# Four chained image layers on one core: when the first image and the constants are loaded, and where PE is given filling matmuls

## The chip, the cores and the metric

The kernel runs on one core of a Trainium2 chip. The metric is the device time of one execution in microseconds (us); smaller is better. The engines are named as the profile names them: PE is TensorE (its weight loads are PEld), DVE is VectorE, ACT is ScalarE, POOL is GpSimd, and SP is SyncE, whose queue issues every DMA of this kernel.

## What is computed

The input `x` holds 32 images of 56 x 56 pixels with 96 channels, float32. Four layers follow each other, and each image goes through them by itself:

```
layer 0   rw = sigmoid(mean over pixels(x) @ Wr + br)            # 4 expert weights for each image
          h  = relu(bn1(x @ (sum of rw[e] * Wpw[e]) + bias))      # 96 -> 384 channels
          h  = relu(bn2(3x3 depthwise(h, sum of rw[e]*Wdw[e])))   # 384 channels
          x  = x + bn3(h @ (sum of rw[e] * Wpwl[e]) + bias)       # 384 -> 96
layer 1   x  = x + 5x5 depthwise(x, a fixed kernel)
layer 2   x  = bn(1x1(3x3 depthwise(relu(x))))
layer 3   shifted-window attention (7x7 windows, 3 heads) and an MLP 96 -> 384 -> 96, both residual
```

## The kernel before

**Stages.** For each image `b` the kernel has four stages: `stage_router` (load the image, mean, expert weights, mixed weights), `stage_conditional` (the rest of layer 0), `stage_depthwise` (layers 1 and 2), and `stage_swin` (layer 3). At step `s` the router of image `s`, the conditional stage of image `s-1`, the depthwise stage of `s-2` and the swin stage of `s-3` are mixed with each other (lines 1469 to 1483). In layer 0, ACT and DVE do the 3x3 depthwise convolution: tap 0 is an ACT copy with a scale, and the other eight are DVE `scalar_tensor_tensor` instructions on 128 x 784 values, called taps below. PE does the 1x1 convolutions, the depthwise convolutions of layers 1 and 2 (as small banded matrices), the transposes, the attention and the MLP.

**The order is planned.** The stages don't issue instructions. They record them in a `Recorder` (line 261). `Recorder.order()` (line 339) then plays the whole program through once with a table of costs (`COST`, line 146) and gives each engine its instructions in the order in which its queue would start them; `give()` (line 482) issues them in that order. On the chip each engine works strictly in that order, and semaphores hold an instruction until its inputs are there and its buffer is free. So what is fixed in advance is the order on each engine, and the times come from the chip.

**Filling matmuls.** Where the plan finds PE without work for over 250 ns (`SPARE_AFTER`, line 161), `order()` puts in a matmul of the 128 x 128 identity with itself into a free PSUM bank (lines 447 to 458). Nobody reads it. It is called a filler below. Each is two MATMUL records in the profile. It waits on the chip, as any matmul does, until the bank that the plan gave it has been read by its last reader. All 8 PSUM banks are one ring.

**The beginning.** `tile_conv_seq_kernel` (line 491) first loads the constants of all four layers and works on them (lines 545 to 714): on SP some 55 loads one after the other, on POOL a dozen memsets and the powers of `rsqrt` (line 558), on DVE the batch-norm factors, the corrections of `band5` (line 640), and those of `pw` and `wo` (lines 652 to 685). The recorded work comes behind all of that on every queue, so the load of the first image (line 732) is issued after the last constant. Scratch space for the constants lies in `h2`, a buffer of layer 0 (line 537).

**The router.** `stage_router` loads an image in one DMA of 1176 KB, and ACT sums it in two passes of 1568 columns each (lines 734 to 737); DVE makes `pooled` and `pooled_w`, PE multiplies with `wr`, and the mixed weights `wmix` follow. The plan puts ACT's passes of images 0 and 1 in the order image 0, image 1, image 0, image 1.

Of the kernel before, what the change touches and what calls it, by code (L numbers as in the profile page):

```python
# [158 lines left out]

TO_TENSOR = {"vector": 1500, "gpsimd": 1500, "scalar": 1000, "sync": 700}  # L160
SPARE_AFTER = 250
SHARING = 1.36


# [96 lines left out]
class Recorder:  # L261
# [77 lines left out]
    def order(self):  # L339
# [66 lines left out]
        def begin(w):  # L406
            nonlocal count
            for b in w.needs:
                if b.slot is None:
                    b.ring.free.sort()  # L410
                    b.slot = b.ring.free.pop(0)[1]
                    b.ring.begun += 1
            result.append(w)
            w.start = now
            e = w.engine
            if e == "gpsimd" or w.calls[0][0] == "scalar_tensor_tensor":
                running[e] = {"work": w, "left": w.ns, "since": now, "rate": 1.0}
                share(now)
                return
            free[e] = now + w.ns  # L420
            heapq.heappush(events, (free[e], count, None))
            heapq.heappush(events, (free[e] + w.landing, count + 1, w))
            count += 2
            if e == "tensor":
                heapq.heappush(events, (free[e] + SPARE_AFTER, count, None))
                count += 1

        left = len(self.work)
        spares = 0
        while left:  # L430
            for e in self.ENGINES:
                if free[e] > now:
                    continue
                held = []
                while queues[e]:
                    item = heapq.heappop(queues[e])
                    w = self.work[item[1]]
                    if not available(w):
                        held.append(item)
                        continue  # L440
                    begin(w)
                    left -= 1
                    if e == "tensor":
                        spares = 0
                    break
                else:
                    if e == "tensor" and self.spare and now >= free[e] + SPARE_AFTER and self.spare[2].free:
                        lhs, rhs, ring = self.spare
                        w = Work(e, 0.0)
                        b = Buffer(ring)  # L450
                        operands = View(b, ring.tiles[0])[:, : rhs.shape[1]], lhs, rhs
                        w.calls.append(("matmul", operands, {"start": True, "stop": True}))
                        w.ns = cost(e, "matmul", operands, {})
                        w.needs, w.starts, w.uses, w.writes = [b], [b], [b], [b]
                        b.users[w], b.left, b.owner = True, 1, w
                        spares += 1
                        assert spares < 10000, "no work can start"
                        begin(w)
                for item in held:
                    heapq.heappush(queues[e], item)  # L460
            assert events, "no work can start"
            now = events[0][0]
            ready = []
            while events and events[0][0] <= now:
                _, _, w = heapq.heappop(events)
                if isinstance(w, tuple):
                    put(w[0])
                elif isinstance(w, dict):

                    if w["end"] == now and running.get(w["work"].engine) is w:  # L470
                        del running[w["work"].engine]
                        w["work"].end = now
                        done(w["work"], now)
                        share(now)
                elif w is not None:
                    done(w, now)
            for v in ready:
                heapq.heappush(events, (v.ready, count, (v,)))
                count += 1
        return result  # L480

    def give(self, tc):
        with tc.manual_schedule():
            for w in self.order():
                for method, args, kw in w.calls:
                    args = [v.found() if isinstance(v, View) else v for v in args]
                    kw = {k: v.found() if isinstance(v, View) else v for k, v in kw.items()}
                    getattr(getattr(self.nc, w.engine), method)(*args, **kw)  # L488
# [3 lines left out]
def kernel(  # L492
# [37 lines left out]
    if general:  # L530
# [2 lines left out]
        tops = ring("top", [PK, NP], 4)  # L533
        dens = ring("den", [PK, NP], 4)


    room = h2s.tiles[0].rearrange("p k n -> p (k n)")
    taken = [0]

    def scratch(rows, n):  # L540
        taken[0] += n
        return room[:rows, taken[0] - n : taken[0]]


    ident = const.tile([P, P], F32, name="ident")
# [2 lines left out]
    nc.gpsimd.memset(ones, 1.0)  # L548
    mhalf = const.tile([P, 4], F32, name="mhalf")
    nc.gpsimd.memset(mhalf, -0.5)  # L550
    mhalves = scratch(P, C)
    nc.gpsimd.memset(mhalves, -0.5)

    def rsqrt(dst, src, eps, scale=1.0):
# [75 lines left out]
    nc.vector.tensor_copy(experts[:, :, 9, :], c384[:, :, V_BPW : V_BPW + E])  # L630
    nc.vector.tensor_copy(experts[:, :, 10, :], c384[:, :, V_BDW : V_BDW + E])


    band5 = load([P, NG, 10, 32], layouts["k5"], "band5")
    centre = scratch(P, 64).rearrange("p (n c) -> p n c", n=2)
    nc.sync.dma_start(out=centre, in_=layouts["centre"])
    for g in range(NG):
        for n in range(2):
            at = 5 * n + 2
            nc.vector.tensor_tensor(band5[:, g, at], band5[:, g, at], centre[:, n], ALU.add)  # L640
    band3 = load([P, NG, 6, 32], layouts["k3"], "band3")


    pw = const.tile([C + 1, CM], F32, name="pw")
    nc.sync.dma_start(out=pw[:C, :C], in_=a["L2_conv_pw_kernel"].rearrange("a b c f -> (a b c) f"))

    def wide(name, keep=False):
        t = const.tile([P, C], F32, name=name) if keep else scratch(P, C)
        nc.sync.dma_start(out=t, in_=a[name].partition_broadcast(P))
        return t  # L650

    inv2 = wide("L2_conv_moving_var")
    rsqrt(inv2, inv2, BN_EPS)
    nc.vector.tensor_tensor(inv2, inv2, wide("L2_conv_gamma"), ALU.mult)
    dwb = scratch(C, P)
    nc.vector.tensor_scalar(dwb, ones[:C].to_broadcast([C, P]), col(U_DWB), None, ALU.mult)
    pt = mm.tiles[4]
    nc.tensor.matmul(pt[:, :C], dwb, pw[:C, :C], start=True, stop=True)
    bias2 = scratch(P, C)
    nc.vector.tensor_tensor(bias2, pt[:, :C], wide("L2_conv_pw_bias"), ALU.add)  # L660
    nc.vector.tensor_tensor(bias2, bias2, wide("L2_conv_moving_mean"), ALU.subtract)
    nc.vector.tensor_tensor(bias2, bias2, inv2, ALU.mult)
    nc.vector.tensor_tensor(bias2, bias2, wide("L2_conv_beta"), ALU.add)
    nc.vector.tensor_tensor(pw[:C, :C], pw[:C, :C], inv2[:C], ALU.mult)
    nc.vector.tensor_copy(pw[C:, :C], bias2[C : C + 1])

    def centre_outputs(w):

# [2 lines left out]
        nc.vector.tensor_scalar(mean, mean, 1.0 / C, None, ALU.mult)  # L671
        nc.vector.tensor_scalar(w[:, :C], w[:, :C], mean, None, ALU.subtract)

    centre_outputs(pw)


    wq = load([C, C], a["L3_conv_wq"], "wq")
    wk = load([C, C], a["L3_conv_wk"], "wk")
    wv = load([C, C], a["L3_conv_wv"], "wv")
    wo = const.tile([C + 1, CM], F32, name="wo")  # L680
    nc.sync.dma_start(out=wo[:C, :C], in_=a["L3_conv_wo"])
    nc.sync.dma_start(out=wo[C:, :C], in_=a["L3_conv_bo"].rearrange("(o c) -> o c", o=1))
    centre_outputs(wo)
    if not general:
        nc.vector.tensor_scalar(wo[:C], wo[:C], -1.0, None, ALU.mult)
    w1 = load([C, M], a["L3_conv_w1"], "w1")
    w2 = load([P, NB, C], a["L3_conv_w2"].rearrange("(k p) f -> p k f", p=P), "w2")
    b2 = wide("L3_conv_b2", True)
    if general:
        masks = load([PK, 2, NP * PK], layouts["mask"].rearrange("l q j k -> q l (j k)"), "masks")  # L690
    else:
        keep_last = load([P, NP, WT], layouts["keep_last"], "keep_last")
        keep_column = load([P, WT], layouts["keep_column"], "keep_column")

        slots = ring("slots", [C, NWIN, SLOT], 3)

        exps = ring("exps", [P, NH, NP, PK], 2)
        for t in slots.tiles + kTs.tiles + exps.tiles:
            nc.gpsimd.memset(t, 0.0)
        ones32 = const.tile([P, HD], F32, name="ones32")  # L700
        nc.gpsimd.memset(ones32, 1.0)

    for t in x1s.tiles + x2s.tiles + [h1.tiles[0] for h1 in h1s]:
        nc.gpsimd.memset(t, 0.0)
    for t in filtereds.tiles + oTs.tiles:
        nc.gpsimd.memset(t[C:], 1.0)

    for t in lnsqs.tiles:
        nc.gpsimd.memset(t[:, :, C:], C * LN_EPS)
    for u in (U_LN1G, U_LN2G):
        nc.vector.tensor_scalar(col(u), col(u), math.sqrt(C), None, ALU.mult)

# [12 lines left out]
    def stage_router(b):  # L728

        xT = chip.new(xTs).part(*range(NROW))  # L730
        sums = new_small("sums", [C, 2])
        chip.sync.dma_start(out=xT, in_=x[b])
        yield 3
        for q in range(2):
            part = xT[:, q * HALF * W : (q + 1) * HALF * W].part(*range(4 * q, 4 * q + 4))
# [733 lines left out]
    for step in range(B + 3):  # L1469
# [11 lines left out]
        if step < B:  # L1481
            stages.append((stage_router(step), 12, when("router", step)))
        interleave(stages)
    chip.give(tc)


def build(nc, shapes, batch):
# [41 lines left out]
```

## Time and profile before

| what | value |
|---|---|
| time, median of 3 runs | 5219.56 us (5214.70 to 5220.35) |
| the profiled execution: time, span | 5218.23 us, 5216.4 us |
| mean clock granted to PE | 0.987 |
| ACT busy | 3841.3 us, 74% |
| POOL busy | 3041.9 us, 58% |
| fillers, MATMUL records, whole span | 1746, in which PE was busy for 249.3 us |
| of these from 0 to 60 us | 100 records, 15.4 us |
| from 60 to 470 us | 684 records, 92.7 us |
| from 470 to 4930 us | 620 records, 95.7 us |
| from 4930 us to the end | 342 records, 45.5 us |

The span is the time from the first to the last instruction of the program on the chip; the execution's own time is 1.8 us longer. A view named "chain of waits" starts at the last instruction and goes back at each step to what released it, or to the instruction before it on its engine. In the timeline a row is a group of equal instructions: start, length, engine, line, operation, `out<-in`, shapes, count, and in brackets how long the engine was idle before and what ended that. Line 488 is the line of `give()` that issues all planned work, so planned instructions are told apart by their tiles: `banks<-ident` is a filler, and `banks<-ident,lnd` is a real transpose. Matmuls are pipelined and their ends are modelled, so PE's busy time is longer than the time between starts.

### The profile page before, as it was taken

The page shows a single profiled execution, that of the slowest core. Times are in us where ns is not written, and L with a number is a line of the kernel's source. Part 1 is how long each engine was busy: PE and PEld are TensorE (multiplying, and loading weights), DVE is VectorE, ACT ScalarE, POOL GpSimd, SP SyncE. Part 2 cuts the span into 40 slices and gives each one's busy share as a digit, 9 for nine tenths or more (in the row PEclk, how much of TensorE's full clock was granted, in tenths as well). Part 3 has the DMA queues.
Part 4 walks back from the last instruction along what each step waited for, and adds up shares of the span by engine and source line. Part 5 has one row for each costly group of instructions (what it writes and reads, how often), then busy time and mean ns, then how long its engine had stood idle before and what let it go on. Part 6 is the DMA issues. An engine that isn't in the chain of part 4 may idle for free.

```text
span 5216.4 us, 139773 instructions
## 1 busy us (share of the span) xinstructions
PE 5044.7 (97%) x58652; PEld 3347.7 (64%) x58652; DVE 4300.9 (82%) x5560; ACT 3841.3 (74%) x7649; POOL 3041.9 (58%) x2432
## 2 busy tenths in 40 slices
PE   5889999999999999999999999999999999999999
PEld 3556666666666666666666666666666666666677
DVE  6887988888988888988888888888888888898722
ACT  2457787777778777777877777877777877777755
POOL 5456755565765555666465665656566555566533
PEclk9899999999999999999999999999999999999999
DMA  1111111111111111101111111111111111110110
GB/s 43 22 27 39 23 28 33 37 36 38 31 25 31 33 39 36 39 20 29 35 37 36 38 27 27 32 36 37 37 34 23 32 33 39 36 39 20 24 28 19
DMA packets 482579, 166.35 MB, mean 32 GB/s; under 512 B 477952, under 2 KB 478613, under 8 KB 478869
## 3 DMA queue, kind: packets, MB, share of 16 engines
q1 hardware_dynamic: 481940, 157.33, 14.7%
q8 instruction: 464, 7.60, 0.6%
q14 instruction: 175, 1.43, 0.1%
HBM read 41.60 MB, written 38.54 MB: 15 GB/s over the span
## 4 chain that ended last, share of the span: by engine, by line
PE 74%; POOL 9%; DVE 6%; ACT 5%; issue 5%; DMA 1%; SPq 0%; DVEq 0%; POOLq 0%; ACTq 0%
PE banks L488 74%; DVE h L488 4%; POOL tb L488 3%; POOL lnd L488 2%; ACT exps L488 2%; POOL xT L488 2%; POOL exps L488 1%; POOL var L488 1%; ACT h L488 1%; ACT hid L488 1%; DVE hid L488 1%; DVE wmix L488 1%; DMA out<-tb 1%; ACT slots L488 0%; DVE res L488 0%
## 5 line engine op out<-in xcount | busy, mean ns | idle before, releaser
L488 DVE SCALAR_TENSOR_TENSOR h<-h,mix,h 128x784 f32<-128x784 f32 x3072 | 3309.9, 1113 | 71.7 <-ACT h L488 56.5
L488 POOL TENSOR_TENSOR var<-var,mhalf 112x4 f32<-112x4 f32 (+1 forms) x512 | 775.4, 1520 | 418.9 <-DVE var L488 409.8
L488 PE MATMUL banks<-x,band 32*32 32x392 f32 x24576 | 851.1, 508 | 0.0
L488 POOL TENSOR_TENSOR xT<-y,xT 96x392 f32<-96x392 f32 x256 | 480.6, 1879 | 491.8 <-ACT y L488 490.5
L488 PE MATMUL banks<-xT,wmix 96*128 96x448 f32 (+1 forms) x1536 | 693.7, 550 | 1.4 <-issue 1.4
L488 ACT ACTIVATE h<-h,biasd,s 128x784 f32<-128x784 f32 x384 | 399.0, 1039 | 348.8 <-DVE h L488 348.6
L488 ACT ACTIVATE hid<-banks,c 128x448 f32<-128x448 f32 (+1 forms) x768 | 437.0, 583 | 287.9 <-PE banks L488 279.5
L488 PEld LDWEIGHTS banks<-w,hid 128*112 128x112 f32 x5376 | 579.9, 182 | 82.0 <-issue 37.8
L488 POOL TENSOR_TENSOR tb<-res 112x384 f32<-112x384 f32 (+1 forms) x256 | 459.8, 1801 | 282.7 <-DMA out<-tb 181.2
L488 PE MATMUL banks<-hT,w 96*128 96x448 f32 (+1 forms) x1536 | 615.5, 502 | 0.2 <-DVE tb L488 0.2
L488 POOL TENSOR_TENSOR lnd<-res,var 112x384 f32<-112x384 f32 (+1 forms) x512 | 590.3, 1159 | 32.8 <-PE banks L488 16.2
L488 ACT ACTIVATE h<-banks,bias,s 128x448 f32<-128x448 f32 (+1 forms) x768 | 539.4, 710 | 90.8 <-PE banks L488 85.0
L488 PE MATMUL banks<-w,hid 128*112 128x96 f32 x5376 | 588.4, 266 | 7.4 <-ACT hid L488 6.4
L488 PE MATMUL banks<-h,wmix 128*96 128x392 f32 x1536 | 560.2, 503 | 17.0 <-ACT h L488 17.0
L488 PEld LDWEIGHTS banks<-x,band 32*32 32x32 f32 x24576 | 407.8, 103 | 247.0 <-issue 161.7
L488 ACT ACTIVATE exps<-banks 49x196 f32<-49x196 f32 x1536 | 507.8, 331 | 40.5 <-PE banks L488 15.8
L488 POOL TENSOR_TENSOR exps<-exps,keep_column 49x147 f32<-49x147 f32 x224 | 207.2, 925 | 479.3 <-ACT exps L488 443.8
L488 PEld LDWEIGHTS banks<-h,wmix 128*96 128x96 f32 x1536 | 245.1, 166 | 258.9 <-issue 210.3
L488 PEld LDWEIGHTS banks<-xT,wmix 96*128 96x128 f32 x1536 | 259.2, 191 | 199.8 <-issue 95.0
L488 ACT ACTIVATE h<-h,mix 128x784 f32<-128x784 f32 x384 | 364.5, 949 | 29.3 <-POOL h L488 21.1
L488 DVE TENSOR_REDUCE var<-lnsq 112x4 f32<-112x388 f32 (+1 forms) x512 | 253.1, 497 | 159.7 <-POOL lnd L488 120.0
L488 PEld LDWEIGHTS banks<-hT,w 96*128 96x128 f32 x1536 | 256.4, 190 | 144.9 <-issue 73.3
(131 smaller groups left out, 7499.6 us busy)
## 6 DMA issues: line engine op xcount, KB each, us to landing
xT<-in_x SPq DMA_DIRECT2D x32, 1176.0 KB
x<-xT SPq DMA_DIRECT2D x384, 98.0 KB
out<-tb SPq DMA_DIRECT2D x128, 168.0 KB
filtered<-x SPq DMA_DIRECT2D x384, 49.0 KB
filtered<-x SPq DMA_DIRECT2D x384, 42.0 KB
out<-tb SPq DMA_DIRECT2D x128, 126.0 KB
filtered<-x SPq DMA_DIRECT2D x384, 7.0 KB
wpw<-in_L_conv_Wpw SPq DMA_DIRECT2D x1, 576.0 KB
```

The source lines that it names most:

```text
L488: getattr(getattr(self.nc, w.engine), method)(*args, **kw)
```

## The change

1. The DMA of image 0 is issued by hand before the constants. The plan gets a stand-in with the same cost (`brought`).
2. The constants of layers 1 to 3 are only named at the beginning. Their loads and the memsets (`first_others`) are issued when the plan reaches 15 us, `rsqrt` of layer 2 (`more_others`) at 45 us, and the remaining DVE work (`last_others`) at 85 us, all from inside `give()`. Scratch for them moves from `h2` to `x3`. The second image's load comes behind the constants of layer 0 and ahead of the other constants.
3. Fillers are planned only after the first real matmul of the plan (`begun`), and those that the plan starts after 450 us are planned, with their banks, and not issued (`SPARE_UNTIL`).
4. The memsets of `h1` come first on POOL.

In the program that is executed the fillers go from 873 to 355: 37 fewer ahead of the router's first matmul and 481 fewer from 450 us of the plan on. The order of everything else is the same on ACT throughout, and on PE, DVE, POOL and SP from the point where the moved constants end. The banks are the same up to one rotation by three.

```diff
+SPARE_UNTIL = 450000
...
-            if e == "gpsimd" or w.calls[0][0] == "scalar_tensor_tensor":
+            if e == "gpsimd" or e == "vector" and w.calls[0][0] == "scalar_tensor_tensor":
...
+        begun = False
...
                     if e == "tensor":
-                        spares = 0
+                        spares, begun = 0, True
...
-                    if e == "tensor" and self.spare and now >= free[e] + SPARE_AFTER and self.spare[2].free:
+                    if e == "tensor" and begun and self.spare and now >= free[e] + SPARE_AFTER and self.spare[2].free:
...
+                        w.n = None
...
+    def brought(self, v):
+
+        w = Work("sync", self.target)
+        w.ns, w.landing = COST["sync", "dma_start"][0], IMAGE_LANDING
+        self.work.append(w)
+        self.touch(w, v, True)
+
-    def give(self, tc):
+    def give(self, tc, others):
+
+        others = sorted(others.items(), reverse=True)
         with tc.manual_schedule():
             for w in self.order():
+                if w.n is None and w.start > SPARE_UNTIL:
+                    continue
+                while others and w.start >= others[-1][0]:
+                    others.pop()[1]()
...
+    nc.sync.dma_start(out=xTs.tiles[0], in_=x[0])
...
+    held = []
+
+    def hold(t, src):
+
+        held.append((t, src))
+        return t
...
+    def first_others():
+        for t, src in held:
+            nc.sync.dma_start(out=t, in_=src)
+        if not general:
+            for t in slots.tiles + kTs.tiles + exps.tiles:
+                nc.gpsimd.memset(t, 0.0)
+            nc.gpsimd.memset(ones32, 1.0)
...
+        for t in x1s.tiles + x2s.tiles:
+            nc.gpsimd.memset(t, 0.0)
...
+    def more_others():
+        rsqrt(inv2, inv2, BN_EPS)
...
+    def last_others():
+        for g in range(NG):
+            for n in range(2):
+                at = 5 * n + 2
+                nc.vector.tensor_tensor(band5[:, g, at], band5[:, g, at], centre[:, n], ALU.add)
+        nc.vector.tensor_tensor(inv2, inv2, gamma2, ALU.mult)
...
+        nc.vector.tensor_tensor(pw[:C, :C], pw[:C, :C], inv2[:C], ALU.mult)
+        nc.vector.tensor_copy(pw[C:, :C], bias2[C : C + 1])
+        centre_outputs(pw)
+        centre_outputs(wo)
+        if not general:
+            nc.vector.tensor_scalar(wo[:C], wo[:C], -1.0, None, ALU.mult)
+
+    others = {15000: first_others, 45000: more_others, 85000: last_others}
...
-        chip.sync.dma_start(out=xT, in_=x[b])
+        if b:
+            chip.sync.dma_start(out=xT, in_=x[b])
+        else:
+            chip.brought(xT)
...
-    chip.give(tc)
+    chip.give(tc, others)
```

## The prediction

> **What bounds the kernel now.** First the page's head and the groups by shape. PE is busy for 97% of the span, DVE for 82%, and 1746 records of PE are fillers:
>
> ```profile
> span 5216.4 us, 139773 instructions
> ...
> PE 5044.7 (97%) x58652; PEld 3347.7 (64%) x58652; DVE 4300.9 (82%) x5560; ACT 3841.3 (74%) x7649; POOL 3041.9 (58%) x2432
> ...
> L488 PE MATMUL banks<-ident 128*128 128x128 f32 x1746 | 249.3, 287 | 58.7 <-ACT h L488 25.9 <-DVE h L660 19.2 <-ACT y L488 12.4
> ```
>
> A busy share that holds filling work doesn't tell what binds, so I read three stretches by themselves: the beginning, a period of the steady middle, and the end.
>
> The beginning, in the timelines of SP, ACT, PE and DVE:
>
> ```profile
> 29.19 0.90 SPq L488 DMA_DIRECT2D xT<-in_x  x2
> 37.10 1.51 ACT L488 ACTIVATE xT<-xT 96x1568 f32<-96x1568 f32 x1 [35.08 <-DMA xT<-in_x]
> ...
> 41.65 1.51 ACT L488 ACTIVATE xT<-xT 96x1568 f32<-96x1568 f32 x1 [2.95 <-DMA xT<-in_x]
> ...
> 43.59 9.65 PE L488 MATMUL banks<-ident 128*128 128x128 f32 x66 [19.15 <-DVE h L660]
> ...
> 46.43 0.28 DVE L488 TENSOR_SCALAR pooled_w<-ones,pooled 96x128 f32<-96x128 f32 x1
> ...
> 58.00 4.47 PE L488 MATMUL banks<-xT,wmix 96*128 96x448 f32 x12 [1.41 <-issue]
> ```
>
> The images are issued at 29.2, after all constants. ACT's second pass is image 1's and waits until 41.65. `pooled_w` is ready at 46.7, but the router's matmul starts only at 53.08: it stands behind 33 fillers, and those had waited for line 660, which waited for the 15.68 us power of line 558. From 62.4 to 126 DVE does 67 taps with 0.1 us of idle time: what starts earlier is earlier.
>
> The middle. The same filler groups return every 309.5 us (two images), so the stretch from 470 to 4930 holds 14.4 periods. The chain of waits from 1310 to 1620 runs through PE for 79.6%, in four pieces:
>
> ```profile
> 1309.91 22.87 PE banks L488 x290
> ...
> 1362.51 16.15 PE banks L488 x111
> ...
> 1397.79 118.35 PE banks L488 x1577
> ...
> 1530.67 89.42 PE banks L488 x1125
> ```
>
> The end, in the timeline:
>
> ```profile
> 5122.09 12.92 PE L488 MATMUL banks<-ident 128*128 128x128 f32 x114
> ...
> 5134.84 3.49 PE L488 MATMUL banks<-pw,filtered 97*112 97x97 f32 x34
> 5135.62 0.40 ACT L488 COPY res<-banks 112x291 f32<-112x291 f32 x1 [16.11 <-PE banks L488]
> ```
>
> 57 fillers run back to back, and the last `pw` matmuls start in the very moment when they are through. ACT has been idle for 16 us by then. The last DMA of `filtered` was issued by 5110.7, and one such DMA on the chain of waits (`out<-tb`) takes 2.31 us: the input was there some 9 us before the fillers began.
>
> **The change, part by part.**
>
> *Beginning.* SP: `gb` ends at 2.2 and the constants begin at 5.8, so image 0 is issued at about 5.8 to 6.2. It lands 7.5 us after its issue (29.6 to 37.1), at 13.7. Behind it all constants are late: the chain of waits shows line 583 at 13.93 waiting for the landing of `wpwl`, and one image ahead costs what the second cost behind the first, 41.65 - 37.10 = 4.5 us. So the last constant of layer 0, before at 18.42, is issued at 22.9, `pw` after it, and image 1 at 23.6. It lands at 31.2 if it takes 7.5 us and at 35.7 if it takes 12 as the second image did; nothing large is ahead of it, so 31.2. ACT does three passes of 1.5 us each, to 34.5 (the fourth isn't needed), DVE's two rows take 0.4, and no filler stands before the router: matmul at 35. From 53.08 to the first expansion at 58.00 were 4.9 us, so expansion at 39.9, which is 18 us earlier. Off that goes 1 us: fillers at this place still ran at 421 ns for a record of 275 and only sped up after 47.8, and now the first expansions are the slow ones. And off goes the DVE work that is moved between the taps, where DVE has no idle time: six `band5` rows 0.70, line 557 0.20, lines 654 to 685 3.6 (42.76 to 46.33): 4.5 us. The 15.68 us power now runs on POOL beside taps. Three taps beside a power (`var`, 1518.65 to 1525.79) took 2.91 us, not stretched; beside a `tb` sum a tap has taken 1.8 us, which would stretch 9 taps by 7 us. It is the same operation as the first row: 0. The memsets (6.2 to 25) and the loads behind image 1 lie in time in which POOL and SP have nothing that the router needs; POOL's three small powers are needed by 36 and come at about 25 to 29, so 7 us of cover. Sum **-13 us**, bounds -18 (no cost) and -1 (image 1 at 35.7, taps stretched).
>
> *Middle.* In a period are nine groups with 20 fillers; from a group's start to the next real matmul it takes 0.24, 0.24, 0.33, 0.47, 0.45, 1.36, 0.92, 0.71 and 0.54 us, 5.26 in all, and all of it would be 14.4 x 5.26 = 76 us. But where the matmul behind a group was waiting anyway, the wait remains: behind the 1.36 at 1432.08, `slots` from ACT ends at 1433.39; behind the 0.71 at 1521.44, `hid` ends at 1522.11. And only what lies in the four pieces of the chain shifts what follows: 0.24 + 0.24 + 0.33 + 0.45 + 0.54 = 1.80, times 14.4 = 26 us.
>
> The fillers also keep the clock up:
>
> ```profile
> 1703.30:1706.70 3.40, 1.41 (x15) 1.00 0.00 0
> 1706.70:1710.10 3.40, 3.40 (x34) 0.50 0.27 54
> ```
>
> These are stretches of 3.4 us with PE's busy time and its granted clock: one wait of 2.76 us (for `lnd`) leaves a stretch at 41% busy, and the next one runs at half clock. That happens once in most periods, for 3.4 or 6.8 us, which costs 1.7 to 3.4. Without fillers a hole of about 1.4 us opens at 1521, with 0.7 more nearby. I take four more drops in the whole middle, 10 us: **-16**. Bounds -76 and, with one more drop in each period, +11.
>
> [...]
>
> *End.* By the same reading, from 4930 on: 12.76 at 5122; 6.37 at 5006 (28 fillers, the `band` matmul behind them needs ACT's copies of 5002.2); 1.2 before that, 3.4 from 5012 to 5053, 3.0 from 5053 to 5117, 4.0 after 5138: 30.7. PE's waits for `oT` and `slots` come to the open here, and I allow three drops of the clock at 2.6 us: 8. **-22**, bounds -41 (all groups) and -12 (the one group at 5122 alone).
>
> Sum: -13 - 16 - 22 = -51. The span becomes 5165, the execution 5167; the median of the runs shown stands 1.3 us above the profiled one, so **5168 us**.
>
> **Rivals.**
>
> *The fillers hid waits.* In the middle the next late engine takes over (ACT's `exps` and POOL's `lnd` already hold the other 20% of the chain): 0 there, -13 - 22: 5185.
>
> *The early image starts nothing.* ACT's order puts image 1 second, so only the second landing counts. With 12 us for it and stretched taps the beginning gives -1: -1 - 16 - 22, 5181.
>
> *The clock holds.* No new drop: -13 - 26 - 31: 5150.
>
> *Slower.* Uncovered holes become half-clock stretches: n more in each period cost 14.4 x 2.6 x n = 37 n. For it speaks that 41% busy was enough, against it that the longest group is 1.36 us. All gains without drops are 70; from 1.9 more stretches per period the change loses. At three, the time is 5220 - 70 + 111 = 5261.
>
> That the order doesn't change the middle at all is no rival: the fillers are gone from it.
>
> **How the numbers follow.** Forecast 0.60; hidden waits 0.17; early image 0.06; clock holds 0.10; slower 0.04; and 0.03 for two of the small cases together, which leaves under 0.2% (about 10 us, what a measurement can tell from no change). Faster 0.93, same 0.03, slower 0.04. The range takes in hidden waits, early image and clock holds with a little of the middle's bound below, 5142 to 5196; the +11 of the middle would give 5195.
>
> **What would show it.** Image 0's DMA at about 6 and image 1's at about 23.6; the first expansion near 40 (not 58); six `band` rows between taps near 95 to 100. The period of the middle about 1 us shorter than 309.5, PE's waits for `lnd` and `hid` longer. From the last tap to the end about 20 us less, with `pw` directly behind the last `wo`. If the period is unchanged, the fillers hid waits; if PE's clock in the middle falls from 0.99 to 0.97 or lower, the holes cost more than I think.

## The result, and the profile after

The changed kernel takes 5217.34 us (median of 13 runs, 5210.96 to 5226.95), the kernel before 5220.2 us (13 runs beside them, 5214.7 to 5226.32). The ratio is 0.9995 with a 95% interval of 0.9987 to 1.0004: the runs can't tell the two kernels apart. The forecast of 5168 us was 49 us too low. The execution that was profiled took 5225.77 us (span 5224.0), 8 us over the median of its kernel, so below I compare stretches and not the two spans.

The page of the changed kernel:

```profile
span 5224.0 us, 137722 instructions
...
PE 5000.7 (96%) x57616; PEld 3276.0 (63%) x57616; DVE 4301.4 (82%) x5561; ACT 3839.3 (73%) x7649; POOL 3000.2 (57%) x2432
...
PE 56%; DVE 16%; ACT 12%; POOL 9%; issue 5%; DMA 1%; SPq 0%; POOLq 0%; ACTq 0%; DVEq 0%
```

Before, the last of these lines (the shares of the chain of waits) was:

```profile
PE 74%; POOL 9%; DVE 6%; ACT 5%; issue 5%; DMA 1%; SPq 0%; DVEq 0%; POOLq 0%; ACTq 0%
```

PE is busy for 44 us less, as the fillers are gone, and the span is no shorter. PE's share of the chain of waits fell from 74% to 56%; DVE has 16% in place of 6%, ACT 12% in place of 5%. Where PE had no filler it now waits, and what it waits for is on the chain.

**The beginning came as forecast.** The timelines of SP, ACT, DVE and PE:

```profile
5.72 0.32 SPq L552 DMA_DIRECT2D xT<-in_x  x1
...
23.16 0.42 SPq L504 DMA_DIRECT2D xT<-in_x  x1
```
```profile
13.79 1.51 ACT L504 ACTIVATE xT<-xT 96x1568 f32<-96x1568 f32 x1 [11.77 <-DMA xT<-in_x]
...
31.24 1.51 ACT L504 ACTIVATE xT<-xT 96x1568 f32<-96x1568 f32 x1 [15.85 <-DMA xT<-in_x]
```
```profile
92.15 2.38 DVE L734 TENSOR_TENSOR band<-band,x 128x32 f32<-128x32 f32 x6
```
```profile
40.99 4.40 PE L504 MATMUL banks<-xT,wmix 96*128 96x448 f32 x12
```

The first expansion starts at 40.99 instead of 58.00, the first tap 17.1 us earlier. The power of line 576 now runs on POOL from 57.18 for 16.40 us beside the taps, and they aren't stretched (1038 ns on average from 40 to 130 us). The moved DVE work costs 5.6 us of the lead, the `band` rows 2.38 of them. Later waits give and take some more, and at image 2 the taps are 14.0 us ahead (images are counted from 0; the recorded expectations below name 16.5 us for image 2, which by this count is image 1).

**Then the lead melts.** Taps of the same number, changed kernel against the kernel before: -14.0 us at image 2, -8.4 at image 7, +1.5 at image 12, +8.2 at image 20, +14.6 at image 31; the last output comes 7.5 us later. So the middle lost 28.6 us in this execution, and the end won 7.1. The windows of PE at two places of a period where it happens, with its busy time and granted clock:

```profile
1388.70:1392.10 3.40, 1.35 (x4) 1.00 0.00 0
1392.10:1395.50 3.40, 2.25 (x13) 0.51 0.00 0
1395.50:1398.90 3.40, 3.40 (x35) 0.50 0.16 31
```
```profile
1518.40:1521.90 3.50, 1.88 (x17) 0.99 0.00 0
1521.90:1525.30 3.40, 3.40 (x18) 0.50 0.02 5
```

and the matmuls behind these holes, in PE's timeline, first before and then in the changed kernel. `lnd` holds the normalised rows of layer 3, which POOL writes and PE transposes; `hid` holds the hidden values of its MLP, which ACT writes. Further down, `slots` holds the rows of the attention's windows (from ACT), and `oT` its result (from DVE).

```profile
1397.79 0.49 PE L488 MATMUL banks<-ident,lnd 112*96 112x112 f32 x3 [2.75 <-POOL lnd L488]
1398.12 1.92 PE L488 MATMUL banks<-w,hid 128*112 128x96 f32 x18
...
1522.15 0.63 PE L488 MATMUL banks<-w,hid 128*112 128x96 f32 x4
```
```profile
1393.25 0.80 PE L504 MATMUL banks<-ident,lnd 112*96 112x112 f32 x3 [3.20 <-POOL lnd L504]
1393.84 3.54 PE L504 MATMUL banks<-w,hid 128*112 128x96 f32 x18
...
1520.23 0.63 PE L504 MATMUL banks<-w,hid 128*112 128x96 f32 x4 [1.13 <-ACT hid L504]
1521.36 3.63 PE L504 MATMUL banks<-w,hid 128*112 128x96 f32 x20 [0.49 <-ACT hid L504]
```

The 18 `hid` records take 3.54 us; before they took 1.92. At the first place this kernel is 4.54 us ahead when the wait for `lnd` ends (1393.25 against 1397.79) and 1.90 when the next `pw` starts (1399.01 against 1400.91): 2.6 us lost. At the second it is 1.92 ahead at the first `hid` (1520.23 against 1522.15) and 0.30 after the group (1525.62 against 1525.92): 1.6 lost.

Added up over the trace's records of the granted clock, PE is at half clock for 58.0 us between 470 and 4930 us before, in 12 stretches, and for 163.8 us in 29 stretches after. Of the 29, 11 stand at the wait for `lnd`, where 12 were before; 13 are new at `hid`, in each of the 13 periods in which that hole of 1.13 us comes; 4 are new at a hole of 1.26 us for `slots`; and one is at 522 us, where the pipeline fills. From 4930 on it is 2.8 us before and 38.2 after. At the end, PE's timeline and windows show a long one behind the wait for `oT`:

```profile
5020.75 1.44 PE L504 MATMUL banks<-wo,oT 97*112 97x97 f32 x6 [2.72 <-DVE oT L504]
```
```profile
5016.90:5020.30 3.40, 1.13 (x14) 1.00 0.00 0
5020.30:5023.70 3.40, 2.95 (x31) 0.53 0.02 5
5023.70:5027.10 3.40, 3.40 (x18) 0.50 0.00 0
5027.10:5030.50 3.40, 3.40 (x30) 0.50 0.00 0
5030.50:5034.00 3.50, 3.50 (x72) 0.50 0.00 0
```

Half clock went on for four such rows although PE was busy for 13.25 of their 13.7 us; the next stretch, from 5140.0, is the longest, 20.5 us. Matched matmul by matmul, the end reads: 15.5 us behind at 5006; 9.5 where the row of 28 fillers was; 14.8 after the first stretch at half clock; 12.2 at 5101; 0.3 ahead where the row of 57 was; 9.1 behind after the second stretch; 7.5 at the last output. The two rows gave 18.6 us and the clock took 14.7 of it.

### The profile page after: what moved, and what is told of

It reads as the page before. It is cut to its first block, busy times and chain, and to the rows that moved or that the text cites. A ratio compares the mean times of both kernels' runs of the same rounds, so it can differ in the third digit from the quotient of the medians.

```text
span 5224.0 us, 137722 instructions
## 1 busy us (share of the span) xinstructions
PE 5000.7 (96%) x57616; PEld 3276.0 (63%) x57616; DVE 4301.4 (82%) x5561; ACT 3839.3 (73%) x7649; POOL 3000.2 (57%) x2432
## 3 DMA queue, kind: packets, MB, share of 16 engines
q1 hardware_dynamic: 481940, 157.33, 14.7%
## 4 chain that ended last, share of the span: by engine, by line
PE 56%; DVE 16%; ACT 12%; POOL 9%; issue 5%; DMA 1%; SPq 0%; POOLq 0%; ACTq 0%; DVEq 0%
PE banks L504 56%; DVE h L504 13%; ACT h L504 4%; POOL tb L504 3%; ACT exps L504 3%; POOL var L504 2%; POOL xT L504 2%; ACT hid L504 1%; POOL lnd L504 1%; DVE wmix L504 1%; DVE hid L504 1%; ACT slots L504 1%; DMA out<-tb 1%; ACT y L504 1%; DVE tb L504 1%
## 5 line engine op out<-in xcount | busy, mean ns | idle before, releaser
L504 POOL TENSOR_TENSOR var<-var,mhalf 112x4 f32<-112x4 f32 (+1 forms) x512 | 786.9, 1542 | 406.0 <-DVE var L504 399.3
L504 POOL TENSOR_TENSOR xT<-y,xT 96x392 f32<-96x392 f32 x256 | 467.1, 1826 | 454.3 <-ACT y L504 453.0
L504 PEld LDWEIGHTS banks<-w,hid 128*112 128x112 f32 x5376 | 600.7, 187 | 100.1 <-issue 38.3
L504 PE MATMUL banks<-w,hid 128*112 128x96 f32 x5376 | 609.4, 272 | 21.6 <-ACT hid L504 21.6
L504 POOL TENSOR_TENSOR lnd<-res,var 112x384 f32<-112x384 f32 (+1 forms) x512 | 525.9, 1033 | 41.1 <-PE banks L504 24.8
L504 DVE TENSOR_TENSOR tb<-banks,tb 112x384 f32<-112x384 f32 (+1 forms) x256 | 128.3, 501 | 273.1 <-PE banks L504 238.7
```

## The experiments

The theory: the missing fillers open holes, each hole costs the clock of the next stretches, and that eats what the beginning and the fillers give. Rival A: the beginning pays nothing, or something other than the fillers eats it. Rival B: the forecast's own sum. A time of "the plan" is one in `order()`'s own play-through. Each ratio is against runs of the kernel before taken beside the variant, whose median went from 5219.2 to 5222.5 us over the four sets; differences of two variants are of their medians.

### Which part does what

`e1_early_start` gives all later fillers again, so that the beginning alone is changed:

```diff
-SPARE_UNTIL = 450000
+SPARE_UNTIL = 450000000
```

> The changed kernel with all of its later fillers given again: only the beginning is changed. In the profile of the changed kernel the taps of image 2 are 16.5 us earlier than before, and this lead is gone by image 20. Theory (fillers kept the clock, and their removal is what eats the lead): with the fillers back nothing eats it, about 5204 us, one stretch at half clock in a period as before, the last taps still 16 us early. Rival A (the beginning pays nothing, because something else than the missing fillers eats the lead, such as the different phase between DVE and POOL): about 5217, the lead shrinks by 2 us in each period as in the changed kernel. Rival B (the forecast's own sum): 13 us under the kernel before, 5207.

Measured 5206.42 us against 5219.24 (ratio 0.9971, 0.9962 to 0.998): 12.8 us less, the forecast's 13. The taps are 12.9 us ahead at image 2 and 12.0 at image 31; half clock in the middle is 58.0 us, as before. Rival A falls.

`e2_no_fillers_in_middle` leaves them out from 450 to 5060 us of the plan, `e3_no_fillers_at_end` from 5060 on:

```diff
+SPARE_AGAIN = 5060000
-                if w.n is None and w.start > SPARE_UNTIL:
+                if w.n is None and SPARE_UNTIL < w.start < SPARE_AGAIN:
```
```diff
-SPARE_UNTIL = 450000
+SPARE_UNTIL = 5060000
```

> The changed kernel with the fillers given again from 5060 us of the plan on (about 4930 us of the profile), so that they are missing in the middle alone. Theory: the middle costs what the trace of the changed kernel shows, a lead of 16.5 us that becomes a lag of 14.6, so 5204 + 31 = 5235, or some 5225 if the profiled execution lost more than most; 29 stretches at half clock in the middle instead of 12. Rival A (the beginning pays nothing and the missing fillers do nothing): 5217. Rival B (the forecast): 13 and 16 us under the kernel before, 5191.

> The changed kernel with the fillers of the middle given again, and those from 5060 us of the plan on left out, so that they are missing at the end alone. Theory: the lead of 16 us stays to the end, and the end gives 7 to 8 us (the trace of the changed kernel: a lag of 14.6 us at the last taps, 7.5 at the last output), so about 5196, the fastest of the four. Rival A: 5209. Rival B (the forecast): 13 and 22 us under the kernel before, 5185.

e2: 5231.47 us (ratio 1.0023, 1.0012 to 1.0033), so the middle alone costs 25.1 us against e1. e3: 5198.19 us (0.9959, 0.9945 to 0.9973), so the end alone gives 8.2. 

`e4_fillers_alone` is the kernel before with the same skipping in `give()` from 450 us on, and the beginning unchanged:

```diff
+SPARE_UNTIL = 450000
...
+                        w.n = None
...
+                if w.n is None and w.start > SPARE_UNTIL:
+                    continue
```

> The kernel before with its beginning unchanged, and with the fillers left out that the plan starts after 450 us. Theory: what the changed kernel loses in the middle and gains at the end, without the lead: 5220 + 31 - 8 = 5243, or some 5233 if the profiled execution of the changed kernel lost more than most. Rival A (the fillers do nothing in the middle): 5220 to 5212. Rival B (the forecast): 38 us under the kernel before, 5182.

Measured 5232.11 us (1.003, 1.0018 to 1.0042): 12.9 us slower than before. Middle and end of e2 and e3 together would be 16.8 slower, the beginning 12.8 faster: the three parts add up to the result within 4 to 6 us. In the profiles the difference lies at the end: there e4 has 10.2 us at half clock ahead of the last 7, and gains 17.8 us from image 31 to the last output, where e3 has 27.3 ahead of the last 4 and gains 9.9. e1 and e3 stand within 3 us of their theory; e2 stands between its two values (5225 and 5235), and e4 at its second (5233), 11 us below the first.

### Is it the clock, and which fillers kept it

`f1_only_the_cover` is e3 with only the six fillers of each period that stand ahead of the `hid` waits; `f2_all_but_the_cover` is e3 without just these six:

```diff
+def cover(t):
+    return 86000 < (t - 1454826) % 318762 < 96000
...
-                if w.n is None and w.start > SPARE_UNTIL:
+                if w.n is None and (w.start > SPARE_UNTIL or w.start > 450000 and not cover(w.start)):
```

(f2 has `and cover(w.start)`.)

> Base: e3_no_fillers_at_end (5198). In the middle only the two filler groups of each period that stand ahead of the matmuls that wait for ACT's hid are kept (six fillers, before at 1515.96 and 1521.44); the other seven groups (14 fillers) are left out. Theory (one group of holes costs the clock, the other fillers are only work): the stretch of 3.4 us at half clock at the hid waits doesn't come; the fillers left out give back up to 26 us as the forecast counted them, and the hole at lnd is longer and costs 6.8 us of half clock in every period instead of in most: 5198 - 26 + 12 = 5184. Rival (what the other fillers took was hidden by the wait for lnd, as the chain of waits would have it where it leaves PE): no gain, and the longer half clock at lnd, so 5198 to 5210.

> Base: e3_no_fillers_at_end (5198). In the middle only these six fillers ahead of the hid waits are left out in each period, the other 14 are kept. Theory: one more stretch of 3.4 us at half clock in each of 14.4 periods, each costing half its length, 1.7 us: 5198 + 24 = 5222. Rival (the clock doesn't set the end; the middle is slower without fillers for another reason): 5198, or a few us less, since six fillers are gone.

Neither theory came true. f1 took 5211.62 us (0.9981, 0.9972 to 0.999), worse than e3 by 13 (11 by the ratios), and above its rival's 5198 to 5210 too. The drop at `hid` is gone, but another came, in six of the 14 periods, where the five fillers of the group at 1432 had stood. Its windows in one of the six:

```profile
1423.70:1427.10 3.40, 2.13 (x36) 1.00 0.66 152
1427.10:1430.50 3.40, 3.40 (x10) 0.50 0.93 214
```

A hole of 1.27 us (for `slots`), in a stretch that was 63% busy, was enough here, with no other idle time beside it. In the changed kernel the same hole of 1.26 us, with 2.14 of 3.40 us busy, cost nothing in the period from 1310 on, and cost the clock in four of the 14.

f2 took 5198.57 us (0.9956, 0.9943 to 0.997), the same as e3 by the medians and what its rival said. Its five runs go from 5197.03 to 5208.07, and the profiled one is the slowest. That one shows the drop at `hid` and 102.4 us of half clock in the middle, and by it f2 is 10 us slower than e3's profiled one; the other four have a higher mean clock (0.981 to 0.982 instead of 0.979; e3's median is 0.983), and no trace shows their drops. So f2 decides nothing alone. f1 shows that no single group kept the clock: three holes in a period can lose it.

The clock records of the traces tell when the same hole loses it. In the traces of the kernel before and of the changed one, each of the 64 and 115 changes of the clock lies on a grid of 3.413 us that runs through the whole execution, to within 0.001 us, so I laid the holes on that grid. The hole for `slots` comes 14 times in the trace of the changed kernel, always 1.26 to 1.27 us long, in a stretch that is 63% busy. In 4 of them it begins 1.57 to 1.94 us into its stretch, and the clock was lost each time; in 10 it begins 0.15 to 0.78 us into it, and the clock was kept each time. In the two traces from 470 to 4930 us, of the grid's stretches at full clock, the clock was lost behind all 19 in which PE was busy for under 48%, behind 22 of the 43 with 48 to 65%, and behind none of the 2485 with more.

That the time goes with the clock can be seen without any edit. Of the 48 runs of the kernel before that were taken beside the variants, the six with a mean clock of 0.988 have a median of 5214.7 us and the seven with 0.985 one of 5226.3: 11.6 us for 0.003 of the mean clock, which is some 31 us at half clock, so 0.37 us for each.

`f3_fillers_at_lnd` is the direct test. It adds fillers to e3 where the largest hole is, into the bank that the waiting transposes fill themselves; nothing is removed:

```diff
+                if w.engine == "tensor" and w.calls[0][0] == "transpose":
+                    if seen % 112 == 53 and 165 <= seen <= 1621:
+                        lhs, rhs, ring = self.spare
+                        for _ in range(8):
+                            dst = ring.tiles[w.calls[0][1][0].buffer.slot][:, :P]
+                            self.nc.tensor.matmul(dst, lhs, rhs, start=True, stop=True)
+                    seen += len(w.calls)
```

> Base: e3_no_fillers_at_end (5198). Fourteen times, once in each period, eight more fillers ahead of the transposes of lnd that leave the hole of 2.75 us, into the bank that these transposes fill themselves. They work inside the hole (8 x 0.23 = 1.8 us) and take nothing from what follows. Theory: the stretches at half clock in the middle (71.7 us in the profile of the base) go to nearly none, and each is worth half its length: 5198 - 36 = 5162 at most; 5172 if part of it falls to other waits. Rival (the clock doesn't set the end, or POOL's lnd chain does): 5198.

Measured 5166.58 us (0.9893, 0.9878 to 0.9909), 31.6 us below e3 (34 by the ratios), between the theory's 5162 and 5172. In the profiled execution PE has not one stretch at half clock in the middle, and the taps gain 24.2 us there where e3 lost 4.0: 28.2 us for 71.7 us of half clock, 0.39 us for each. The wait in e3, and then PE's timeline and windows in f3:

```profile
1381.90 0.79 PE L504 MATMUL banks<-ident,lnd 112*96 112x112 f32 x3 [2.74 <-POOL lnd L504]
```
```profile
1374.19 1.95 PE L507 MATMUL banks<-ident 128*128 128x128 f32 x16
1377.11 0.49 PE L512 MATMUL banks<-ident,lnd 112*96 112x112 f32 x3 [0.97 <-POOL lnd L512]
1377.44 1.92 PE L512 MATMUL banks<-w,hid 128*112 128x96 f32 x18
```
```profile
1376.20:1379.60 3.40, 2.49 (x33) 1.00 0.03 5
1379.60:1383.00 3.40, 3.40 (x74) 1.00 0.54 107
```

The 2.74 us of e3's wait are now 1.8 of fillers and 0.97 of waiting, `hid` runs at 1.92 us, and `lnd` comes no later for it. The clock of the kernel before fell at the same place, so this gain was probably open to it as well; it was not run.

### The end, and what the fillers themselves cost

`f4_long_rows_cut` is e1 with at most six fillers in a row after 450 us:

```diff
+                if w.engine == "tensor":
+                    row = row + 1 if w.n is None else 0
-                if w.n is None and w.start > SPARE_UNTIL:
+                if w.n is None and w.start > 450000 and row > 6:
                     continue
```

> Base: e1_early_start (5206, all later fillers given). Of any row of fillers after 450 us at most six are given, which cuts the row of 57 at the end to 6 and the row of 28 to 6 and touches hardly anything else. Theory: the clock is kept at the end (6 us at half clock instead of the 31.6 of e3), the work of 51 and 22 fillers at 0.226 us is gone as far as it was on the path, 11.5 and up to 5: about 5206 - 16 = 5190, that is, better than leaving all of them out (5198). Rival (at the end the clock costs nothing, the fillers alone do): 5198 or more, since some fillers are left.

Measured 5192.31 us (0.9942, 0.9929 to 0.9956), with 5.6 us at half clock from 4930 on: cutting the long rows is worth 14 us where leaving out every filler is worth 8. The theory had 5190.

`g1_lnd_and_long_rows` is f3 with this end. `g4_lnd_and_end` is f3 (no filler of the plan at the end) with 21 fillers set by hand at five holes there, named by the plan's time in us (the loop that issues `more` fillers into the bank of the matmul behind them is left out here):

```diff
+HOLES = {5142: 8, 5278: 3, 5281: 2, 5318: 4, 5320: 4}
...
+                    b = w.calls[0][1][0].buffer
+                    more = HOLES.get(round(w.start / 1000), 0) if b in w.starts else 0
...
```

> f3_fillers_at_lnd (5167) with the end of f4_long_rows_cut: fillers are given at the end too, no more than six in a row. Theory: the two are in different places and add up, f4 stood 6 us below e3: 5161. Rival (with the middle at full clock the end is bound by something else): 5167.

> f3_fillers_at_lnd (5167; none of the plan's fillers at the end) with 21 fillers by hand ahead of the five matmuls at the end whose holes stand ahead of the two drops of the clock: eight at the wait of 2.72 us for oT, then 3, 2, 4 and 4. Theory: some 30 us at half clock go to the few behind the last matmul, worth half: 5167 - 13 = 5154, and this is 22 us for the end against e1_early_start's fillers, what the forecast said for it. Rival (the waits at the end hide the slower clock): 5167.

g1: 5162.5 us (0.9885, 0.9868 to 0.9901), 4.1 us below f3, where f4 stood 5.9 below e3: the two nearly add up. g4: 5155.34 us (0.9872, 0.9856 to 0.9889), 11 us below f3, where the theory had 5154. The clock at the end is held (5.4 us instead of 35.1), and from image 31 to the last output g4 gains 24.1 us on the kernel before; f3 gained 11.2, e1 1.3. So 12.9 us for 29.7 us of half clock, 0.43 for each.

`g2_lnd_and_covers_only` is f3, with ten fillers at `lnd`, without the nine fillers of a period that stand ahead of none of the three holes; `h2_best_without_on_path` is g4 with the same:

```diff
+def cover(t):
+    t = (t - 1454826) % 318762
+    return t < 2500 or 86000 < t < 96000
...
-                if w.n is None and w.start > SPARE_UNTIL:
+                if w.n is None and (w.start > SPARE_UNTIL or w.start > 450000 and not cover(w.start)):
```

> f3_fillers_at_lnd (5167) with ten fillers at lnd in place of eight, and with the fillers of the middle left out except for the three groups that stand ahead of a wait (before at 1432.08, 1515.96 and 1521.44). Now no stretch at half clock comes in either kernel, so that this measures what the nine other fillers of a period (1321.36 to 1375.09 and 1586.05) cost by themselves. Theory (from the lag of f1, f2 and of the changed kernel against their time at half clock, the work of all 20 fillers is worth some 16 us of the 26 that the forecast counted, of which 10 are these): 5157. Rival (forecast): 5167 - 26 = 5141. Rival (hidden waits): 5167.

> g4_lnd_and_end (5155) with ten fillers at lnd and without the nine fillers of each period that stand ahead of no wait that cost the clock (before at 1321.36 to 1375.09 and 1586.05), as g2 without the end's drops. Forecast's price for them: 26 us, so 5129. Theory after g2 (5 us by the medians, 2 us in the middle of the profiled execution): the waits for lnd behind them grow by what they leave, 5150 to 5153. If nothing at all: 5155.

g2: 5161.31 us (0.9886, 0.9867 to 0.9905), 5.3 below f3. h2: 5149.56 us (0.9863, 0.9846 to 0.9879), 5.8 below g4 and the fastest of all, 1.4% below the kernel before and 1.3% below the changed one. The forecast had 26 us for these fillers; by the medians 5 to 6 are there.

The profiles put the price at 6 to 7.5 us. Matched matmul by matmul, g2 gains 6.1 us on f3 between 600 and 4900 us, and h2 gains 7.5 on g4. The expectation that no stretch at half clock comes didn't hold: two rows of fillers from the filling of the pipeline are missing too, and behind them g2 has 13.7 us at half clock (from 522 us on) that cost 2.7 us, and h2 23.9 us (from 523 and 564 on) that cost 7.2. At the end, where f3 and g2 are the same, f3's profiled execution has 30.7 us at half clock ahead of the last few and g2's 13.7, so the difference of f3 and g2 need not be the fillers' alone. h2's profiled execution is the slowest of its four (5158.48, the others 5148.04 to 5151.03).

Where the rest of the 26 us is can be read from the waits. The group at 1359.20 took 0.47 us before; the wait for `lnd` behind it, first before, then in the changed kernel:

```profile
1362.51 0.59 PE L488 MATMUL banks<-ident,lnd 112*96 112x112 f32 x4 [0.41 <-POOL lnd L488]
```
```profile
1357.95 0.59 PE L504 MATMUL banks<-ident,lnd 112*96 112x112 f32 x4 [0.86 <-POOL lnd L504]
```

It is longer by what the group left, and so is the one behind the group at 1375.09 (2.75 to 3.20). Averaged over the periods of the traces of g4 and h2, the groups at 1359.20 and 1375.09 give 0.45 and 0.44 us, and the next wait for `lnd` takes all of it back; the groups of 1321 to 1327 give 0.61, of which 0.30 is lost again within some 15 us; the group at 1586.05 gives 0.45, of which 0.35 is lost within the next 20 us. Less than half a us of 1.95 stays in each period, and 13 periods of it make the 6 us.

`h1_four_at_lnd` is g4 with four fillers at `lnd` instead of eight:

```diff
-                            more = 8
+                            more = 4
```

> g4_lnd_and_end (5155) with four fillers instead of eight ahead of the transposes of lnd: they take 0.9 us, and some 1.85 us of the hole of 2.75 us stay open. It tells how large a hole the clock stands here. If what counts is that the hole stays under about half of a stretch of 3.4 us (in the trace of before, stretches at 41% busy lost the clock, and holes of 1.1 to 1.3 us lost it only where more idle time lay beside them): the clock drops in part of the periods, 5155 to 5165. If any hole over 1.3 us costs the clock: it drops in all 14, as in e3, 28 us more, 5183. If four are enough: 5155.

Measured 5160.43 us (0.9883, 0.9867 to 0.99), 5 above g4. A hole of 1.88 us stays, and in the profiled execution the clock falls at 3 of the 14: the first of the three expectations. The first of the three, in PE's windows:

```profile
764.20:767.60 3.40, 1.56 (x16) 1.00 0.00 0
767.60:771.00 3.40, 3.40 (x34) 0.50 0.33 70
```

Here one stretch takes nearly the whole hole: 1.56 of its 3.40 us are busy. A grid of 3.413 us continued from 771.0 has a boundary near 1382.0, so the hole of the same 1.88 us that ends at 1382.92 lies across two stretches, some 1.0 us in the first and 0.9 in the second, and there the clock was kept. (The expectation's remark that holes of 1.1 to 1.3 us lost the clock only where more idle time lay beside them isn't so: see the hole of 1.27 us in f1.)

### All in one table

From the profiled executions: what the taps lose (+) or gain (-) against the kernel before between image 2 and image 31, what is won from there to the last output, and the time at half clock in each.

| kernel | median, us | middle | half clock 470 to 4930 | end | half clock from 4930 |
|---|---|---|---|---|---|
| before | 5220 | 0 | 58.0 | 0 | 2.8 |
| e1 beginning alone | 5206.4 | +0.9 | 58.0 | -1.3 | 6.0 |
| e2 no fillers in the middle | 5231.5 | +25.5 | 160.4 | +0.8 | 4.0 |
| e3 none at the end | 5198.2 | +4.0 | 71.7 | -9.9 | 31.6 |
| after | 5217.3 | +28.6 | 163.8 | -7.1 | 38.2 |
| f3 cover at `lnd` | 5166.6 | -24.2 | 0 | -11.2 | 35.1 |
| g4 and at the end | 5155.3 | -23.7 | 0 | -24.1 | 5.4 |

## Why the prediction was wrong, step by step

**Beginning, -13: right.** e1 gives -12.8. Image 0's DMA at 5.72, image 1's at 23.16, the expansion at 40.99, no stretched taps: each step stood where it was put. One row was too small: the six `band` rows took 2.38 us and not 0.70, and the moved DVE work cost 5.6 us and not 4.5. *The early image starts nothing* is refuted.

**Middle, -16: wrong in both terms; it is +25 (e2 against e1).** The step that failed first is "I take four more drops in the whole middle, 10 us". There were 17 more, and 106 us more of half clock in the profiled execution. The text had seen the hole ("a hole of about 1.4 us opens at 1521"), and measured the loss at one hole of 2.76 us, but no row gave the number four: it set its price as if smaller holes were nearly harmless. That hole lost the clock in each of the 13 periods in which it came. The second step that failed is "0.24 + 0.24 + 0.33 + 0.45 + 0.54 = 1.80, times 14.4 = 26 us". It took every group inside a piece of the chain on PE as work that shifts the end; but a chain names one releaser at each step, and behind each group the next waits took back between half and all of what it left. What remains is 6 to 7.5 us (g2, h2). So the period became some 2 us longer (28.6 us over 14.4 periods) where the text had it 1 us shorter. The rival *The fillers hid waits* was largely right about the work, and *Slower* about the clock, at a lower price and with less on the other side: it put a drop at 2.6 us, and here 17 drops cost some 31 (25, and the 6 of work that was given back), 1.8 each. They are 1.2 in each period, below the 1.9 that I gave as the point from which the change loses; but of the 70 us of gains in that point some 20 of the middle and 9 of the end weren't there, and the end lost another 15 to the clock.

**End, -22: wrong by the clock.** It is -8 (e3 against e1). The rows of 57 and 28 gave 18.6 us of the 19.1 counted for them, while of the other 11.6 some 3 came. "I allow three drops of the clock at 2.6 us: 8" was the failed term: ahead of the last few us there were two, 10 to 14 us and 17 to 20 us long, that cost 14.7. With the clock held by hand the end gives what the forecast said (g4: -24.1 in the profile, -22.8 against e1). That g4 and h2 come out near the rival *The clock holds* (5150) is chance in the middle: the 24 us there are drops of the kernel before that were covered, not work of fillers.

**The price of the holes.** I had seen one wait of 2.76 us lose the clock, and priced the new holes of the middle at only 10 us. In the runs less was enough: holes of 1.13 and 0.49 us next to each other lost the clock, and one of 1.27. The price I gave a stretch at half clock, half of its length (1.7 of 3.4 us, an estimate from the granted 0.50), is the upper end: f3 and g4 show 0.39 and 0.43 of the time at half clock, and the middle of e2 against e1 some 0.30 (31 us for 102.4).

**The alarm was too coarse.** "If PE's clock in the middle falls from 0.99 to 0.97 or lower": it fell to 0.98. Over 4460 us, one hundredth of the mean clock is 89 us at half clock, and at 0.4 us for each that is some 36 us, more than the whole term it was to guard.

What stays open: why a hole late in its stretch of the grid lost the clock and the same hole early in it, at the same 63% busy, did not. Why a `band` row took 0.40 us between taps was not tried.

## What to carry to other kernels

Work that nobody reads can still carry the clock (leaving out the fillers of the middle cost 25.1 us here): before it is taken out, look up the busy share and clock of every stretch that it filled, on the grid on which the clock changed (3.413 us here) and in many periods, since a hole moved against that grid from one period to the next (the one for `slots` began 1.57, 0.15, 0.55, 0.76 and 1.89 us into its stretch in the first five). Price the loss by the time at half clock (0.3 to 0.4 us for each us here), not by a count of drops. Here filling work paid where PE waits anyway, put into the bank that the waiting matmul will fill: 14 times eight fillers at one wait gained 31.6 us, while the same kind of fillers in rows of 28 and 57 cost 14. A removed piece of work on the chain is worth only what the next wait leaves of it; follow it to that wait before multiplying by the number of periods.

## What was not expected of the hardware

- A hole far shorter than a stretch of 3.4 us lost the clock: 1.27 us (f1), or 1.13 and 0.49 us (changed kernel).
- Half clock went on while PE was busy nearly all the time: 13.7 us at 5020.3 (13.25 of them busy) and 20.5 us at 5140.0 (19.7 busy) in the changed kernel, against 3.4 or 6.8 us in 28 of the 29 places of the middle.
- In the traces of the kernel before and of the changed one, all 179 changes of the clock lie on a grid of 3.413 us, and the same hole lost it or kept it by where it fell on that grid: 1.26 us for `slots`, 4 of 4 lost late in a stretch (1.57 to 1.94 us into it) and 0 of 10 early in it (0.15 to 0.78). At `lnd`, the hole of 1.88 us in h1 lost the clock in 3 of 14. It fits this that executions of one kernel differ: f2's runs go from 5197.03 to 5208.07 us with a mean clock of 0.979 in the slowest and 0.981 to 0.982 in the others.
- With the clock held in middle and end, DVE is busy for 83% and PE still has 73% of the chain of waits (g4), so that PE binds for most of the span at full clock too.
